# One exponential over two neighbouring PSUM banks, fewer fourth maxima and a longer lead in an attention kernel on one core

## The chip, the cores and the metric

The kernel runs on one core of a Trainium2 chip. The core has five engines that work side by side and meet at semaphores: PE (TensorE: matrix products into PSUM), DVE (VectorE), ACT (ScalarE: exponentials and other functions), POOL (GpSimd) and SP (SyncE, which issues the transfers here). PSUM has eight banks of 512 float32 columns on each of 128 partitions. The metric is the device time of one execution in microseconds (us), the median of several runs.

## The reference

Two transformer layers over 4096 rows of 256 features, 16 heads of 16. Layer 0: a block-sparse attention (each block of 128 queries sees its own 128 keys and every eighth key of the whole sequence) and a product quantised to 8 bits. Layer 1: two full causal attentions, one with rotary positions, one with normalised queries and keys, and a mixture of four experts behind the second. What bears on the change is the softmax of the causal attentions:

```python
scores = jnp.einsum('bhqd,bhkd->bhqk', Q, K) / math.sqrt(Dh)
scores = jnp.where(causal, scores, jnp.finfo(scores.dtype).min)
attn = jax.nn.softmax(scores, axis=-1)
y = jnp.einsum('bhqk,bhkd->bhqd', attn, V)
```

## The kernel before

**Units and tiles.** The 4096 queries are cut into 8 chunks of 512 (`ch`), the 16 heads into 4 groups of 4 (`g`). There are three attentions (`a`: 0 is layer 0's sparse one, 1 and 2 are layer 1's). A *unit* is one (a, g, ch). For a = 1 and 2 it runs over the keys in *tiles* of 128, 4 (ch + 1) of them; for a = 0 it has 5 tiles (four of strided keys, one of local keys).

**Scores.** In a tile the scores of the four heads stand as keys x queries, 128 x 512, each in a PSUM bank `st`. The four are made in two groups, p = 0 and p = 1, of two heads each (j = 0 and 1). Head j uses rows 64 j to 64 j + 63 of the PE array, so that the two run side by side. The softmax's row maximum is subtracted in the product itself: the first tile of a unit adds rows with the negated maxima (`pick`, `rows`), and for a = 1 and 2 the later tiles add the product with the *difference* of the keys to those before (`ke` from `e_d`). So the scores of a tile are made on top of those of the tile before, in the same bank. Each of the four banks is held for the whole unit, and a tile's product into it must await the exponential that reads the tile before. ACT makes the exponentials into SBUF tiles `pt`, 12 buffers, one instruction for each head (line 1300 in `exponentials`, 1278). `values` (1352) multiplies a tile's four `pt` with V into `po`, with 32 columns of the array for each head; in the order of the program it stands after both score groups of the next tile.

**Maxima.** The row maxima come from a second, transposed product, queries x keys, into banks `pm`, which DVE reduces to `mx`: one 128 x 512 reduction for each (query block, head, key chunk). They are made ahead, for later units, by the class `Maxima` (1098): within a score group up to two are put beside the scores, one in each half of the array (`exponentials` calls `pick` and `begin`; `emit`, 1040, takes from the two halves in turn, own scores first in the upper and last in the lower half). What isn't ready when a unit starts is made by `complete` (1232). In the stretches of the experts (`between`) `after` (1221) puts in maxima by fours.

**Who may go when.** The program's order on each engine is written out by a planner. `Clock` follows PE, DVE and ACT with prices for each operation; `pick` (1158) takes a maximum if its bank will be free, by this clock, no later than a `slack` after it could begin. `patience` (1204) gives the slack: 0.7 us if more than 2.9 maxima for each tile are still to be done in the next units, else 0.1. `LEAD` (1102) bounds how many units ahead of the one started maxima may belong to. The work of preparing and of the experts is a list with keys that say beside which tile it stands.

**PSUM.** Three rings: `max` with 3 banks, `bank` with 4, `acc` with 1 (`po`). Scores stand in `bank`; maxima beside scores in `max`; products of the preparation in `bank` unless a unit holds it, then in `max`; the experts' in `max` and the maxima beside them in `bank`. `reserve` (119) drains what is open in a ring before it hands out banks. The lines of nearly all instructions in the profile are L87, the helper that keeps the order, so groups are known by their tiles.

Of the kernel before, what the change touches and what calls it, by code (L numbers as in the profile page):

```python
# [101 lines left out]
class Schedule:  # L102
# [4 lines left out]

    RINGS = {"max": 3, "bank": 4}  # L110

    def __init__(self):
        self.items, self.n = [], 0
        self.opened = {ring: [] for ring in self.RINGS}
        self.held = 0
        self.after = None
        self.dense = False

    def reserve(self, ring, banks):
        held = self.held if ring == "bank" else 0  # L120
        while len(self.opened[ring]) + held + banks > self.RINGS[ring]:
            self.opened[ring].pop(0)[1]()

    def hold(self, banks):
        self.held += banks
# [15 lines left out]
    def run(self):  # L141
        opened = self.opened
        while self.items or any(opened.values()):
            due, ring0 = min(((min(due for due, _ in o), r) for r, o in opened.items() if o), default=(None, None))
            if not self.items or (due is not None and due <= self.items[0][0]):
                opened[ring0].pop(0)[1]()
                continue
            _, _, (ring, banks, fn, drain) = heapq.heappop(self.items)
            if ring is not None:
                ring = self.free_ring(ring)  # L150
                self.reserve(ring, banks)
            fn()
            if drain is not None:
                opened[ring].append(drain)
            self.after()


# [1 line left out]
def tile_two_layers(ctx: ExitStack, tc, d, out):  # L159
# [24 lines left out]

    sched = Schedule()

    def bank_tile(name, ring=None):
        ring = ring or sched.free_ring()
        return ps[ring].tile([P, CW], F32, tag=ring, name=name)

    def load(name, shape, dtype=F32, pool=const, src=None, eng=None):
# [23 lines left out]


    with ExitStack() as at:
        psum(at, 0, max=3, bank=4, acc=1)
        c1 = at.enter_context(tc.tile_pool(name="c1", bufs=1))
        work = at.enter_context(tc.tile_pool(name="work", bufs=1))  # L220
        clock = Clock()
# [372 lines left out]
        def prepare1(ch):  # L594
# [81 lines left out]
            for what, n, wcol, dst in (("k", 3, 1, k_d[2]), ("q", 4, 0, q_d[2])):  # L676
                z = {}
                name = what + "2"

                def mm2(tp, z=z, name=name, n=n):  # L680
                    z[tp] = bank_tile(f"p{name}{tp}{nm}").rearrange("p (t n) -> p t n", t=2)
                    for j in range(2):
                        t = 2 * tp + j
                        for c in range(2):
                            pe.matmul(
                                z[tp][:, j, :], s["ht"][:, c, t * P : (t + 1) * P],
                                w[n][:, c, :], start=(c == 0), stop=(c == 1),
                            )

                def sq2(tp, z=z, name=name):  # L690
                    if tp == 0:
                        z["raw"] = work.tile([P, TPC, E], F32, tag="xt" if name == "k2" else "cs", name=f"raw_{name}{nm}")
                        z["ss"] = small.tile([P, TPC * H], F32, tag="ss2", name=f"ss2_{name}{nm}")
                        z["rs"] = small.tile([P, TPC * H], F32, tag="rs2", name=f"rs2_{name}{nm}")
                    act.copy(z["raw"][:, 2 * tp : 2 * tp + 2], z[tp])
                    sq = work.tile([P, 2 * E], F32, tag="r1", name=f"sq2_{name}{tp}{nm}", bufs=2)
                    act.square(sq, z[tp].rearrange("p t n -> p (t n)"))
                    ss = z["ss"][:, 2 * H * tp : 2 * H * (tp + 1)]
                    dve.tensor_reduce(ss, sq.rearrange("p (h d) -> p h d", d=D), AX.X, ALU.add)

                def norms2(z=z, name=name):


                    x, y = z["ss"], z["rs"]
                    e = small.tile([P, TPC], F32, tag="ne2", name=f"ne2_{name}{nm}")
                    dve.tensor_scalar(e, s["ms"], RMS_EPS, None, ALU.mult)
                    t = small.tile([P, TPC * H], F32, tag="nt2", name=f"nt2_{name}{nm}")
                    xv = x.rearrange("p (t h) -> p t h", h=H)
                    over = e.unsqueeze(2).to_broadcast([P, TPC, H])
                    dve.scalar_tensor_tensor(xv, xv, 1.0 / D, over, ALU.mult, ALU.add)  # L710
                    dve.tensor_scalar(y.bitcast(I32), x.bitcast(I32), 1, None, ALU.logical_shift_right)
                    dve.tensor_scalar(y.bitcast(I32), y.bitcast(I32), -1, 0x5F3759DF, ALU.mult, ALU.add)
                    for _ in range(3):
                        dve.tensor_tensor(t, x, y, ALU.mult)
                        dve.scalar_tensor_tensor(t, t, -0.5, y, ALU.mult, ALU.mult)
                        dve.scalar_tensor_tensor(y, t, 1.5, y, ALU.add, ALU.mult)

                def mul2(z=z):
                    v = z["raw"].rearrange("p t (h d) -> p (t h) d", d=D)
                    dve.tensor_tensor(v, v, z["rs"].unsqueeze(2).to_broadcast([P, TPC * H, D]), ALU.mult)  # L720

                def ev2(half, pt, z=z, wcol=wcol, name=name):
                    z[half, 0] = work.tile([P, CW], F32, tag="r0", name=f"n_{name}{half}{nm}", bufs=2)
                    act.activation(z[half, 0], pt, AF.Copy, scale=qkw[:, wcol : wcol + 1])

                def st2(half, z=z, dst=dst, what=what, name=name):
                    split_stored(z[half, 0], dst, half, ch * CW, what, f"{name}{half}{nm}")

                products = [
                    (lambda tp=tp, f=mm2: f(tp), "bank", lambda tp=tp, f=sq2: f(tp)) for tp in range(2)  # L730
                ]
                turns, stores = [], []
                turn(turns, lambda z=z: z["raw"], ev2, f"pt{name}{nm}")
                for half in range(2):
                    act_piece(stores, lambda half=half, f=st2: f(half))
                    if what == "k":
                        act_piece(
                            stores, lambda half=half, z=z: steps_stored(z[half, 0], 2, ch, half, f"2{half}{nm}")
                        )
                rest.append((products, norms2, mul2, turns, stores))  # L740
# [65 lines left out]
        def experts(ch):  # L806
# [97 lines left out]

            def activated(to, func):
                def drain(f, p):
                    t = work.tile([P, CW], F32, tag="pt", name=f"h_{nm}{to}{f}", bufs=12)
                    act.activation(t, p, func)
                    s[to, f] = t

                return drain

# [185 lines left out]
        class Maxima:  # L1098


            HEADS = (1, 0, 3, 2)
            LEAD = 5

            def __init__(self):
                self.units, self.at, self.k_at, self.started = [], 0, 0, 0
# [98 lines left out]
            def patience(self, u, kt):  # L1204
# [2 lines left out]
                todo = sum(len(v["todo"]) for v in self.units[self.at : u["no"] + 1])  # L1207
                for v in self.units[u["no"] + 1 : u["no"] + 4]:
                    todo += len(v["todo"])
                    if todo > 2.9 * max(tiles, 1):  # L1210
                        return 0.7
                    tiles += (TPC * v["keys"] if v["a"] else TPC + 1) + v["spare"]
                return 0.1
# [32 lines left out]

        def neg(u):

            u["neg"] = small.tile([P, TPC * HPG], F32, tag="nm", name="nm_" + u["nm"], bufs=7)
            dve.tensor_reduce(  # L1250
                u["neg"], u["mx"][:, :, :, 0 : u["keys"]].rearrange("p t h c -> p (t h) c"), AX.X, ALU.max, negate=True
            )
# [25 lines left out]
        def exponentials(u, kt, p, lo, make, key):  # L1278
# [2 lines left out]
            if picked:  # L1281
                sched.reserve("max", len(picked))
            side, ends = stream.begin(picked, "max")
            if not u["a"]:
                sched.reserve("bank", 2)
                st = [bank_tile(f"st_{u['nm']}_{kt}_{2 * p + j}", "bank") for j in range(2)]
            elif kt == 0:
                sched.reserve("bank", 2)
                sched.hold(2)
                st = u["st", p] = [bank_tile(f"st_{u['nm']}_{2 * p + j}", "bank") for j in range(2)]  # L1290
            else:
                st = u["st", p]
            if u["a"] and kt == TPC * (u["ch"] + 1) - 1:
                sched.hold(-2)
            clock.pe = max(clock.pe, bank_ends[p])
            own = [make(st[j], j, half_rows(j)) for j in range(2)]
            emit(own[0] + side[0], side[1] + own[1])
            for j in range(2):
                pt = work.tile([P, CW], F32, tag="pt", name=f"pt_{u['nm']}_{kt}_{2 * p + j}", bufs=12)
                act.activation(pt[:, lo:], st[j][:, lo:], AF.Exp)  # L1300
                u[kt, 2 * p + j] = pt
                clock.act = max(clock.act, clock.pe + 0.2) + 0.05 + 0.43 * (CW - lo) / CW
                if j == 0:
                    bank_ends[p] = clock.act
            stream.finish(ends)

        def causal_exp(u, kt, p, key):
# [478 lines left out]
```

## Time and profile before

| | |
|---|---|
| median of 3 runs | 4914.74 us (4911.92 to 4918.79) |
| profiled execution, its own time | 4919.01 us |
| its span | 4917.2 us |
| mean granted clock of PE | 0.966 |
| PE busy | 4615.4 us |
| DVE busy | 3692.0 us |
| ACT busy | 3095.2 us, of it exponentials of scores 2581.0 in 5248 |
| PE's idle time before maxima (`pm_a`) | 135.4 us, 103.5 of it ended by DVE |
| PE's idle time before scores (`st_a`) | 31.3 us, 20.2 of it ended by ACT |

Busy time is the union of an engine's instructions; those of PE overlap each other, and the ends that the profile gives them are modelled, so a busy PE may still be waiting for part of that time. Idle time is put down to the instruction that ended it. `pt_a<-st_a` are the exponentials, `st_a<-qe_a,ke_a` the scores, `pm_a<-km_a,qm_a` the products for the maxima, `mx_a<-pm_a` their reductions, `po_a<-pt_a,v` the value products. A value product shows as two instructions for each head, eight for each tile.

### The profile page before, as it was taken

How to read it: one execution, taken by the hardware profiler on the slowest of the kernel's cores; microseconds unless marked ns; L12 is line 12 of the kernel's file. 1: busy time of each engine (PE TensorE's matmuls, PEld its weight loads, DVE VectorE, ACT ScalarE, POOL GpSimd, SP SyncE). 2: the span in 40 equal slices, each digit the busy share in tenths (PEclk: the TensorE clock that was granted, in tenths of full speed). 3: DMA queues.
4: the chain of work that ended last, by engine and by line, in shares of the span. 5: the costliest groups of instructions: out<-in, count | busy, mean ns of one | idle time of the engine just before them, and what ended most of it. 6: DMA issues, size and time to landing. Idle time of an engine off the chain costs nothing.

```text
span 4917.2 us, 83614 instructions
## 1 busy us (share of the span) xinstructions
PE 4615.4 (94%) x30176; PEld 2291.5 (47%) x30176; DVE 3692.0 (75%) x8399; ACT 3095.2 (63%) x6234; POOL 970.2 (20%) x1637
## 2 busy tenths in 40 slices
PE   6988899999999999999999999999999989999999
PEld 3544454554454445444454444444444434444435
DVE  4776687687767887888888887788887888887811
ACT  2555463477267734788358885488684678585782
POOL 2444413222222132111321103101002100000000
PEclk8988899999999999999999999999999999999999
DMA  6757656554655465444654444544344434333422
GB/s 207 233 198 271 211 188 219 192 183 167 202 176 175 163 209 176 163 160 145 216 185 150 166 145 167 183 141 159 125 148 165 170 127 148 124 131 107 132 87 77
DMA packets 532470, 822.85 MB, mean 167 GB/s; under 512 B 87380, under 2 KB 196436, under 8 KB 532056
## 3 DMA queue, kind: packets, MB, share of 16 engines
q1 hardware_dynamic: 529456, 816.12, 49.6%
q8 instruction: 239, 3.92, 0.3%
q10 hardware_dynamic: 2600, 1.39, 0.1%
q14 instruction: 175, 1.43, 0.1%
HBM read 636.45 MB, written 180.91 MB: 166 GB/s over the span
## 4 chain that ended last, share of the span: by engine, by line
PE 74%; DVE 11%; issue 6%; POOL 4%; DMA 3%; ACT 1%; SPq 0%; ACTq 0%; POOLq 0%; DVEq 0%
PE po_a L87 22%; PE st_a L87 20%; PE pm_a L87 14%; DVE mx_a L87 5%; DVE pm_a L87 3%; PE pe_m L87 2%; PE pp L87 2%; PE pq L87 2%; PE pk L87 2%; PE pv L87 1%; POOL x L87 1%; PE ph_m6l L87 1%; PE ph_m3l L87 1%; PE ph_m2l L87 1%; PE ph_m7l L87 1%
## 5 line engine op out<-in xcount | busy, mean ns | idle before, releaser
L87 ACT ACTIVATE pt_a<-st_a 128x512 f32<-128x512 f32 (+3 forms) x5248 | 2581.0, 572 | 667.0 <-PE st_a L87 423.0
L87 DVE TENSOR_REDUCE mx_a<-pm_a 128x1 f32<-128x512 f32 (+1 forms) x3712 | 2331.7, 684 | 498.5 <-PE pm_a L87 333.4
L87 PE MATMUL pm_a<-km_a,qm_a 64*128 64x512 f32 (+3 forms) x5632 | 1835.7, 432 | 135.4 <-DVE mx_a L87 103.5
L87 PE MATMUL st_a<-qe_a,ke_a 64*128 64x512 f32 (+3 forms) x5632 | 1607.6, 405 | 31.3 <-ACT pt_a L87 20.2
L87 PEld LDWEIGHTS st_a<-qe_a,ke_a 64*128 64x128 f32 x5632 | 865.2, 188 | 1072.4 <-ACT pt_a L87 963.5
L87 PE MATMUL po_a<-pt_a,v 128*32 128x512 f32 (+3 forms) x11264 | 1334.6, 552 | 0.0
L87 PEld LDWEIGHTS pm_a<-km_a,qm_a 64*128 64x128 f32 x5632 | 857.9, 189 | 528.6 <-DVE mx_a L87 370.2
L87 DVE CUSTOM_DVE_ANT_0 pm_a<-pm_a,never_sb 128x512 f32<-128x512 f32 (+3 forms) x1024 | 478.1, 518 | 231.5 <-PE pm_a L87 167.2
L87 POOL CAST rows<-tu_a 8x128 fp32r<-8x128 f32 x768 | 224.2, 292 | 1400.4 <-PE st_a L87 1023.8
L87 DVE CUSTOM_DVE_ANT_0 pm_a<-pm_a,hidden_sb 128x512 f32<-128x512 f32 x512 | 339.4, 719 | 95.4 <-PE pm_a L87 76.3
L87 PEld LDWEIGHTS po_a<-pt_a,v 128*32 128x32 f32 x11264 | 228.7, 108 | 365.5 <-issue 331.9
L87 PE MATMUL st_a<-rows,pick_r 64*128 64x512 f32 x896 | 320.5, 426 | 7.4 <-POOL rows L87 7.3
L87 POOL TENSOR_TENSOR om_a<-od_a,rd_a 128x256 f32<-128x256 f32 x96 | 60.7, 632 | 886.7 <-DVE rd_a L87 779.1
L87 PE MATMUL st_a<-mcol_sb,identb_sb 64*128 64x128 bf16 (+1 forms) x2048 | 234.9, 211 | 0.0
L87 DVE DVE_READ_ACCUMULATOR2_ANT mx_a<- 128x1 f32 x1536 | 218.3, 142 | 0.0
L87 PEld LDWEIGHTS st_a<-rows,pick_r 64*128 64x128 f32 x896 | 164.1, 193 | 18.2 <-POOL rows L87 9.0
L87 DVE STREAM_TRANSPOSE od_a<-oc_a 128x256 f32<-128x256 f32 x192 | 83.3, 434 | 90.1 <-ACT oc_a L87 89.6
L87 DVE SCALAR_TENSOR_TENSOR acc_m<-pe_m,g_wt_m,acc_m 128x192 f32<-128x192 f32 x128 | 51.5, 412 | 108.3 <-PE pe_m L87 107.6
L87 PEld LDWEIGHTS <-identb_sb 64*128 64x128 bf16 x2048 | 109.6, 97 | 19.4 <-issue 3.2
L87 POOL CAST pad<-nm_a 128x16 fp32r<-128x16 f32 x96 | 21.1, 219 | 438.1 <-DVE nm_a L87 436.8
L87 POOL TENSOR_TENSOR xa<-xa,pa 128x512 f32<-128x512 f32 (+1 forms) x48 | 57.0, 1187 | 221.0 <-ACT pa L87 138.8
L87 ACT CAST hl_e<-step 128x512 fp32r<-128x512 f32 x32 | 19.8, 618 | 126.3 <-POOL step L87 121.4
(409 smaller groups left out, 3818.3 us busy)
## 6 DMA issues: line engine op xcount, KB each, us to landing
km_a<-k_d SPq DMA_DIRECT2D x352, 512.0 KB, 3.7
ke_a<-e_d SPq DMA_DIRECT2D x288, 512.0 KB, 5.0
k_d<-hl_k SPq DMA_DIRECT2D x100, 512.0 KB, 4.4
q_d<-hl_q SPq DMA_DIRECT2D x96, 512.0 KB, 4.7
qm_a<-q_d SPq DMA_DIRECT2D x96, 512.0 KB, 5.6
qe_a<-q_d SPq DMA_DIRECT2D x96, 512.0 KB, 5.5
v<-v_d SPq DMA_DIRECT2D x352, 136.0 KB, 5.0
ke_a<-k_d SPq DMA_DIRECT2D x64, 512.0 KB, 6.0
```

What stands on the lines that cost most here:

```text
L87: got = emit(*args, **kw)
```

## The change

- The ring `bank` becomes two tiles of two neighbouring banks each (`pair_tile`). The scores of a group's two heads stand in one pair, and one ACT instruction over [128, 2, 512] makes both exponentials, into one SBUF pair `pt` (6 buffers of two instead of 12 of one). Others take a pair's halves one after the other (`bank_tile`); a half that is left when scores take a new pair is skipped. The experts' activations write into halves of a pair, too.
- `reserve` counts tiles made instead of banks held.
- The planner's price for the exponentials of a group is 0.05 + 0.79 us for 512 columns, and both banks are free at its end; it was 0.05 + 0.43 for each, and the group's banks counted as free after the first.
- `patience` gives 0.7 us only in the first two chunks of queries, and 0.1 us in all others.
- `LEAD` is 7 instead of 5, with 9 buffers for the negated maxima instead of 7. A small scratch vector of the preparation (`nt2`) has one buffer instead of two.

```diff
-    RINGS = {"max": 3, "bank": 4}
+    RINGS = {"max": 3, "bank": 2}
...
-    def reserve(self, ring, banks):
-        held = self.held if ring == "bank" else 0
-        while len(self.opened[ring]) + held + banks > self.RINGS[ring]:
-            self.opened[ring].pop(0)[1]()
+        self.made = dict.fromkeys(self.RINGS, 0)
+        self.half = None
+
+    def reserve(self, ring, banks, whole=False):
+
+        opened, new = self.opened[ring], banks
+        if ring == "bank":
+            new = 1 if whole else (banks - (self.half is not None) + 1) // 2
+        while opened and opened[0][2] + self.RINGS[ring] < self.made[ring] + new:
+            opened.pop(0)[1]()
...
+    def pair_tile(name):
+        sched.made["bank"] += 1
+        sched.half = None
+        return ps["bank"].tile([P, 2, CW], F32, tag="bank", name=name)
+
     def bank_tile(name, ring=None):
         ring = ring or sched.free_ring()
+        if ring == "bank":
+            if sched.half is None:
+                pair = pair_tile(name)
+                sched.half = pair[:, 1]
+                return pair[:, 0]
+            bank, sched.half = sched.half, None
+            return bank
+        sched.made[ring] += 1
         return ps[ring].tile([P, CW], F32, tag=ring, name=name)
...
-                    t = small.tile([P, TPC * H], F32, tag="nt2", name=f"nt2_{name}{nm}")
+                    t = small.tile([P, TPC * H], F32, tag="nt2", name=f"nt2_{name}{nm}", bufs=1)
...
-                    t = work.tile([P, CW], F32, tag="pt", name=f"h_{nm}{to}{f}", bufs=12)
-                    act.activation(t, p, func)
-                    s[to, f] = t
+                    if f % 2 == 0:
+                        t = work.tile([P, 2, CW], F32, tag="pt", name=f"h_{nm}{to}{f}", bufs=6)
+                        s[to, f], s[to, f + 1] = t[:, 0], t[:, 1]
+                    act.activation(s[to, f], p, func)
...
-            LEAD = 5
+            LEAD = 7
...
-                    if todo > 2.9 * max(tiles, 1):
+                    if u["ch"] < 2 and todo > 2.9 * max(tiles, 1):
                         return 0.7
...
-            u["neg"] = small.tile([P, TPC * HPG], F32, tag="nm", name="nm_" + u["nm"], bufs=7)
+            u["neg"] = small.tile([P, TPC * HPG], F32, tag="nm", name="nm_" + u["nm"], bufs=9)
...
-            if not u["a"]:
-                sched.reserve("bank", 2)
-                st = [bank_tile(f"st_{u['nm']}_{kt}_{2 * p + j}", "bank") for j in range(2)]
-            elif kt == 0:
-                sched.reserve("bank", 2)
-                sched.hold(2)
-                st = u["st", p] = [bank_tile(f"st_{u['nm']}_{2 * p + j}", "bank") for j in range(2)]
-            else:
-                st = u["st", p]
+            if not u["a"] or kt == 0:
+                sched.reserve("bank", 2, True)
+                u["st", p] = pair_tile(f"st_{u['nm']}_{kt}_{p}")
+                sched.hold(2 if u["a"] else 0)
+            st = u["st", p]
...
-            own = [make(st[j], j, half_rows(j)) for j in range(2)]
+            own = [make(st[:, j], j, half_rows(j)) for j in range(2)]
             emit(own[0] + side[0], side[1] + own[1])
+            pt = work.tile([P, 2, CW], F32, tag="pt", name=f"pt_{u['nm']}_{kt}_{p}", bufs=6)
+            act.activation(pt[:, :, lo:], st[:, :, lo:], AF.Exp)
             for j in range(2):
-                pt = work.tile([P, CW], F32, tag="pt", name=f"pt_{u['nm']}_{kt}_{2 * p + j}", bufs=12)
-                act.activation(pt[:, lo:], st[j][:, lo:], AF.Exp)
-                u[kt, 2 * p + j] = pt
-                clock.act = max(clock.act, clock.pe + 0.2) + 0.05 + 0.43 * (CW - lo) / CW
-                if j == 0:
-                    bank_ends[p] = clock.act
+                u[kt, 2 * p + j] = pt[:, j]
+            bank_ends[p] = clock.act = max(clock.act, clock.pe + 0.2) + 0.05 + 0.79 * (CW - lo) / CW
             stream.finish(ends)
```

More of the change, by code (lines that the diff above doesn't have):

```diff
@@ L143, in run @@
         while self.items or any(opened.values()):
-            due, ring0 = min(((min(due for due, _ in o), r) for r, o in opened.items() if o), default=(None, None))
+            due, ring0 = min(((min(due for due, _, _ in o), r) for r, o in opened.items() if o), default=(None, None))
             if not self.items or (due is not None and due <= self.items[0][0]):
@@ L153, in run @@
             if drain is not None:
-                opened[ring].append(drain)
+                opened[ring].append((*drain, self.made[ring] - 1))
             self.after()
@@ L217, in tile_two_layers @@
     with ExitStack() as at:
-        psum(at, 0, max=3, bank=4, acc=1)
+        psum(at, 0, max=3, bank=2, acc=1)
         c1 = at.enter_context(tc.tile_pool(name="c1", bufs=1))
```

## The prediction

> **What bounds the kernel now.** I read the page's busy times first, then the groups by shape, then the timeline of single tiles, and last the order in which the instructions of both programs are built.
>
> The page's first part:
>
> ```profile
> PE 4615.4 (94%) x30176; PEld 2291.5 (47%) x30176; DVE 3692.0 (75%) x8399; ACT 3095.2 (63%) x6234; POOL 970.2 (20%) x1637
> ```
>
> PE is busy 94%, but its records overlap and include waiting, so I look at the unit of work: the *tile* of 128 keys x 512 queries x four heads. A tile is a first score group E0 (pair p=0), a second, E1 (p=1), and the value products PV of the tile before. There are 1312 of them; from one E0 to the next they add up to 4900 of the 4917 us. First a tile with four maxima, then two tiles with three (PE's timeline in two stretches; start, length, both us):
>
> ```profile
> 4000.62 0.49 PE L87 MATMUL st_a<-qe_a,ke_a 64*128 64x512 f32 x1
> 4000.63 0.72 PE L87 MATMUL pm_a<-km_a,qm_a 64*128 64x512 f32 x2
> 4000.97 0.61 PE L87 MATMUL st_a<-qe_a,ke_a 64*128 64x512 f32 x2
> 4001.20 0.39 PE L87 MATMUL pm_a<-km_a,qm_a 64*128 64x512 f32 x1
> 4002.13 0.50 PE L87 MATMUL pm_a<-km_a,qm_a 64*128 64x512 f32 x1 [0.55 <-DVE mx_a L87]
> 4002.13 0.50 PE L87 MATMUL st_a<-qe_a,ke_a 64*128 64x512 f32 x1
> 4002.56 1.06 PE L87 MATMUL po_a<-pt_a,v 128*32 128x512 f32 x8
> 4003.56 0.51 PE L87 MATMUL st_a<-qe_a,ke_a 64*128 64x512 f32 x1
> ...
> 3221.30 0.49 PE L87 MATMUL st_a<-qe_a,ke_a 64*128 64x512 f32 x1
> 3221.31 0.72 PE L87 MATMUL pm_a<-km_a,qm_a 64*128 64x512 f32 x2
> 3221.64 0.79 PE L87 MATMUL st_a<-qe_a,ke_a 64*128 64x512 f32 x3
> 3222.10 0.39 PE L87 MATMUL pm_a<-km_a,qm_a 64*128 64x512 f32 x1
> 3222.42 1.07 PE L87 MATMUL po_a<-pt_a,v 128*32 128x512 f32 x8
> 3223.41 0.50 PE L87 MATMUL st_a<-qe_a,ke_a 64*128 64x512 f32 x1
> 3223.42 0.73 PE L87 MATMUL pm_a<-km_a,qm_a 64*128 64x512 f32 x2
> 3223.76 0.62 PE L87 MATMUL st_a<-qe_a,ke_a 64*128 64x512 f32 x2
> 3224.00 0.49 PE L87 MATMUL pm_a<-km_a,qm_a 64*128 64x512 f32 x1
> 3224.34 0.39 PE L87 MATMUL st_a<-qe_a,ke_a 64*128 64x512 f32 x1
> 3224.66 1.06 PE L87 MATMUL po_a<-pt_a,v 128*32 128x512 f32 x8
> ```
>
> Above, four maxima: the fourth finds its bank taken until a reduction ends, and the fourth score matmul and PV stand behind it; the tile lasts 2.94 us. Below, three maxima: PE never pauses in the first of them (2.11 us) and loses some 0.1 us in the second (2.25; its third maximum, at 3224.00, also waits for DVE). The full tiles (512 columns, nothing else in them) of the trace, by number of maxima: none, 48, mean 2.07; three, 663, mean 2.19, median 2.12; four, 61, mean 2.87. So PE bounds the tile of three, DVE the tile of four (four reductions of 0.68). ACT is the reserve; its part of a tile, from its timeline, and then two rows of the groups by shape (busy us, mean ns):
>
> ```profile
> 4004.10 2.07 ACT L87 ACTIVATE pt_a<-st_a 128x512 f32<-128x512 f32 x4 [0.80 <-PE st_a L87]
> ```
>
> ```profile
> L87 ACT ACTIVATE pt_a<-st_a 128x512 f32<-128x512 f32 x4480 | 2334.0, 604 | 528.4 <-PE st_a L87 339.5 <-PE pm_a L87 166.8
> L87 ACT ACTIVATE pt_a<-st_a 128x128 f32<-128x128 f32 x256 | 59.2, 278 | 56.2 <-PE pm_a L87 33.0 <-PE st_a L87 21.5 <-ACT pt_a L87 0.5
> ```
>
> Four exponentials take 2.07 us end to end; a column costs (604-278)/384 = 0.85 ns, 0.435 us for 512.
>
> **The change, part by part.** The sum is made on the profiled run: 4919.0 us, span 4917.2 and 1.8 around it; the median of the runs is 4.3 us lower.
>
> *No fourth maximum (patience) and lead 7.* The built orders tell where maxima move. Full tiles with none: 48 to 29; three: 663 to 742; four: 61 to 8; six and more: 16 to 11; the number of tiles is the same, 794. At the means of before (2.07, 2.19, 2.87, 2.97 for six, 3.44 for seven, 3.72 above) the 794 cost 1791 us before and 1752 after: 39 us less. First tiles of units (with row products) go 108 to 108, four maxima 82 to 79, nine and more 8 to 5: by their means (2.82 and 4.85) 5 us less; the masked tiles +3. Together **-41 us**. The maxima don't vanish: 54 fourth ones go into 19 tiles at the end that had none, where PE had room (ACT-bound, 2.07). The lead alone has no other price: more units begun means the q and k loads on SP are issued earlier, and km_a loads ended only 18.5 us of PE's idle time. Bounds: 30 us (if a freed tile costs 2.3) to 45.
>
> *One exponential for two heads.* ACT does 2624 instead of 5248. It saves one start per pair: pitch in the run of four (2.07-0.60)/3 = 0.49, minus 0.435, = 0.055 us; 145 us of ACT's time, but ACT has 0.8 us to spare in the tile above, so none of it is on the path. What counts is when a pair's banks come free. Before: the first exponential starts 0.53 after E0 (4003.56 to 4004.10), as soon as head 0's scores are done, and each bank is free for the next tile when its own exponential ends: E1's first bank 1.58 later, 2.11 after E0. After: (1) the exponential must await head 1's scores too, which stand behind a maximum in their half of the array and end 0.73 after E0 (3221.64+0.39-3221.30). (2) In the built order 2370 of the 2624 stand behind a separate wait instruction on ACT (their own buffer's last writer is a second wait; before, 1614 of 5248). In the trace an exponential that found ACT idle starts 36 ns (median of 449) after the scores' end without it and 95 ns (median of 460) with it: start 0.83. (3) Two instructions of 1024 take 2.07-0.11 = 1.96: end 2.79. (4) PE resumes 0.05 after an exponential's end (4690.75 to 4690.81 where a tile has no maxima). So **E1's first weight load of the next tile can start 2.84 after E0, where before it could at 2.16.** It is wanted at E0 + 2.18 + 0.57 - 0.11 = 2.64 (tile of three, offset of E1, weights loaded ahead). It is late by 0.2 us, and behind it in PE's order stand the maximum, head 3's scores, PV and the next E0. The late start also costs the 0.11 of loading ahead (a score matmul that begins on its weights lasts 0.50, else 0.39). From E1's late start to the E0 after it: 0.66 to PV, 1.00 to E0, 1.66. The loop spans two tiles: 2.84+1.66 = 4.50, 2.25 a tile, against 2.11 and 2.25, mean 2.18, before. DVE's 0.1 us in every second tile is swallowed by it. Price 0.06 x 635 tiles (323 and 312 of the two orders) = 40 us. For 97 full tiles whose maxima are narrower PE is faster (medians 2.08 and 2.00), E0's scores end at 0.62, the loop is (2.72+1.64)/2 = 2.18: 0.13 x 97 = 13 us. Tiles of none: 29 x -0.04 = -1. Strided, first and masked tiles have more in E0 and E1 or shorter exponentials; their E1 comes later than the release, price 0. Together **+52 us**.
>
> Bounds: below, 0 (the release is in time) less the 1 us; above, if the pair saves nothing on ACT (2.07), loop (2.95+1.66)/2 = 2.30: 76 + 18 = 94. I take 52, made of the nearest rows.
>
> The rule that speaks against the pair is in the Trainium skill, "ScalarE: Activation LUTs", What ACT_TABLE_LOAD costs: an ACTIVATE with immediate scale takes 186 ns + 0.833 ns a column, and back-to-back ones overlap by 93. The rows give 0.85 and about 0.17 fixed. By the page a pair's two would take 1.985, the loop 2.26 and the price some 61 us (an estimate): merging buys only the overlap's remainder, and delays the first half by a whole stream.
>
> *Banks in neighbouring pairs.* A preparation's product alone uses half a pair, and the next scores skip the other half. The units of layer 0 beside which products are prepared (32 tiles) may wait for an eviction more; the next scores already waited for the last exponential there: 0 to 10 us, I take 2. In the experts' stretches maxima go by fours, two pairs, and the second issued waits as before for the second reduction; six fours begin in half a pair and then wait for one of their own, at most 1.2 each, 7 us; the same stretches lose nothing else: -2 (DVE hides some) to 7, I take 2. The experts' activations write halves of a pair, as many and as long: PE's four matmuls of 0.6 hide them; were they late, one activation of 0.6 a layer. The smaller pool for one small vector and two more of another: DVE orders them itself, 0.
>
> Sum: -41 + 52 + 4 = **+15 us**: profiled 4934, median 4930.
>
> **Rivals.**
> (a) *The wait is hidden, the kernel is faster.* If the release comes by 2.64 after E0 instead of 2.84, PE is never late, and only the tiles of four count: -41 to -30, 4874 to 4885. For it: the 0.2 us rests on the start 0.30 later and a sum of four durations; PE already loses 0.1 in every second tile. Against: 0.06 of it is a wait that the order shows in nine of ten pairs. It decides from E1's weight load waiting less than 0.05 us.
> (b) *Heavier.* A pair takes as long as two and DVE's wait adds to the loop: +94-30 = +64, 4979.
> (c) *They cancel*: price 30 to 50 in the loop, gain 41: within 10 us.
>
> A change smaller than 0.2% (10 us) cannot be told from none here.
>
> **How the numbers follow.** (a) 0.30. (c) 0.20. My forecast's upper part and (b), a net loss over 10 us, 0.50. The likeliest is 4930; its own range is 4912 to 4955. The range goes from (a), 4874 less the 4 of the sum's rest, to most of (b): 4870 to 4970. Signs: faster 0.30, same 0.19, slower 0.51.
>
> **What the changed profile would show.** Full tiles of four nearly gone, PE's idle time before pm_a down from 135 us: right on the first part. Exponentials of 128x1024 at about 1.03 us, 0.83 after E0. If I am right on the second, E1's first score matmul lasts 0.50 instead of 0.39 in most tiles of three, its weight load ended by ACT pt_a, and the median of these tiles is 2.23 to 2.27. If it stays at 2.12 to 2.18, rival (a). Wrong altogether: a stage of prep or experts that changes by over 10 us.

## The result, and the profile after

| | before | after |
|---|---|---|
| median, run side by side | 4913.51 us (4 runs) | 5046.91 us (4 runs, 5042.75 to 5055.29) |
| profiled execution / its span | 4919.0 / 4917.2 us | 5046.0 / 5044.2 us |
| PE / ACT busy | 94% / 63% | 92% / 58% |

The kernel is slower: ratio 1.0272 (95% interval 1.0254 to 1.029), +133 us where the forecast was +15 (ratio 1.003, the range 4870 to 4970 us).

The first part of the page of after, and from its groups the exponentials, the products for the maxima, the scores, and the scores' weight loads (busy us, mean ns | idle time before them and what ended most of it):

```profile
PE 4658.3 (92%) x30176; PEld 2190.4 (43%) x30176; DVE 3714.1 (74%) x8399; ACT 2925.8 (58%) x3610; POOL 968.6 (19%) x1637
...
L87 ACT ACTIVATE pt_a<-st_a 128x1024 f32<-128x1024 f32 (+3 forms) x2624 | 2408.7, 961 | 893.2 <-PE st_a L87 639.8
...
L87 PE MATMUL pm_a<-km_a,qm_a 64*128 64x512 f32 (+2 forms) x5631 | 1865.1, 435 | 184.8 <-DVE mx_a L87 151.2
L87 PE MATMUL st_a<-qe_a,ke_a 64*128 64x512 f32 (+3 forms) x5632 | 1628.9, 416 | 59.8 <-ACT pt_a L87 40.1
L87 PEld LDWEIGHTS st_a<-qe_a,ke_a 64*128 64x128 f32 x5632 | 803.3, 188 | 1262.4 <-ACT pt_a L87 1094.6
```

ACT does 172 us less for the scores (2581.0 to 2408.7) and the kernel gains nothing from it. PE's idle time before maxima went from 135.4 to 184.8 us, although the fourth maxima are nearly gone; before scores from 31.3 to 59.8. So there are two new waits, one on DVE and one on ACT. To see where they are, the trace is cut into tiles, and the times from one first score to the next are added by kind of tile. The order in which each kernel was built tells which instruction belongs to which tile, so the counts differ a little from the prediction's. (us, rounded; one profiled execution of each kernel; the third column is the kernel before with patience and lead 7 alone, the run e3_pick_lead below. The expectations below give the ten stretches as 1344 and 1428 us, by another cut.)

| kind of tile | before | patience and lead, single banks | after |
|---|---|---|---|
| full tiles (814) | 1869 | 1838 | 1883 |
| first tiles of units and first masked tiles, 512 columns (102) | 293 | 294 | 292 |
| other masked tiles (172) | 373 | 370 | 372 |
| attention 2 with other work beside (23) | 144 | 143 | 144 |
| attention 1 with other work beside (31) | 156 | 153 | 151 |
| layer 0 (a = 0), with the start ahead of it | 746 | 737 | 763 |
| the ten longest stretches of the experts, with the end | 1338 | 1339 | **1438** |
| span | 4917 | 4873 | 5044 |

The full tiles did nearly what the prediction said. The experts' stretches, which it gave 2 us, take 100 us more.

**The pair's wait in the full tile.** PE's timeline of after over two tiles of three maxima (start, length, both us):

```profile
2314.25 0.50 PE L87 MATMUL st_a<-qe_a,ke_a 64*128 64x512 f32 x1
2314.25 0.73 PE L87 MATMUL pm_a<-km_a,qm_a 64*128 64x512 f32 x2
2314.59 0.73 PE L87 MATMUL st_a<-qe_a,ke_a 64*128 64x512 f32 x3
2315.16 0.39 PE L87 MATMUL pm_a<-km_a,qm_a 64*128 64x512 f32 x1
2315.48 1.06 PE L87 MATMUL po_a<-pt_a,v 128*32 128x512 f32 x8
2316.47 0.49 PE L87 MATMUL st_a<-qe_a,ke_a 64*128 64x512 f32 x1
...
2317.20 0.46 PE L87 MATMUL pm_a<-km_a,qm_a 64*128 64x512 f32 x1
...
2318.83 0.50 PE L87 MATMUL st_a<-qe_a,ke_a 64*128 64x512 f32 x1
```

ACT's timeline and that of PE's weight loads in the same stretch:

```profile
2315.11 1.94 ACT L87 ACTIVATE pt_a<-st_a 128x1024 f32<-128x1024 f32 x2 [0.35 <-PE st_a L87]
```

```profile
2317.10 0.18 PEld L87 LDWEIGHTS st_a<-qe_a,ke_a 64*128 64x128 f32 x1 [0.33 <-ACT pt_a L87]
```

The two tiles last 2.22 and 2.36 us. The first pair of exponentials begins 0.86 after E0 (2315.11 - 2314.25) and both end at 2317.05, 2.80 after E0; E1's first weights in the next tile start 0.05 later. Here the chain of the prediction can be read link by link. In 427 of the 643 tiles with three maxima of full width E1's first score matmul now lasts about 0.50; before, in 8 of 562.

**The new wait in the experts' stretches.** PE's timeline of after there, and the reductions of the four maxima in its middle:

```profile
1924.63 1.99 PE L87 MATMUL pq<-w,ht 128*128 128x256 f32 x8
1926.55 0.73 PE L87 MATMUL pm_a<-km_a,qm_a 64*128 64x512 f32 x3
1927.84 0.49 PE L87 MATMUL pm_a<-km_a,qm_a 64*128 64x512 f32 x1 [0.56 <-DVE mx_a L87]
1928.26 3.70 PE L87 MATMUL ph_m2l<-h_m2l,w_l 128*128 128x512 f32 x8
1931.89 0.73 PE L87 MATMUL pm_a<-km_a,qm_a 64*128 64x512 f32 x3
1933.17 0.49 PE L87 MATMUL pm_a<-km_a,qm_a 64*128 64x512 f32 x1 [0.55 <-DVE mx_a L87]
```

```profile
1927.09 2.48 DVE L87 TENSOR_REDUCE mx_a<-pm_a 128x1 f32<-128x512 f32 x4 [1.15 <-PE pm_a L87]
```

Of four maxima three go, and the fourth waits: the first reduction starts at 1927.09 and takes 0.68, and at 1927.84 the fourth begins. The four occupy PE from 1926.55 to 1928.26, 1.71 us. Where they pass without a wait they take 0.66, as here in the same stretch of before (1848.31 - 1847.65):

```profile
1847.65 0.73 PE L87 MATMUL pm_a<-km_a,qm_a 64*128 64x512 f32 x4
1848.31 1.57 PE L87 MATMUL pe_m<-w_e0d,h_m2e 128*128 128x192 f32 x8
```

### The profile page after: what moved, and what is told of

Same layout as the page of the kernel before. It is cut to its first block, busy times and chain, and to the rows that moved or that the text cites. A ratio compares the mean times of both kernels' runs of the same rounds, so it can differ in the third digit from the quotient of the medians.

```text
span 5044.2 us, 81693 instructions
## 1 busy us (share of the span) xinstructions
PE 4658.3 (92%) x30176; PEld 2190.4 (43%) x30176; DVE 3714.1 (74%) x8399; ACT 2925.8 (58%) x3610; POOL 968.6 (19%) x1637
## 4 chain that ended last, share of the span: by engine, by line
PE 71%; DVE 13%; issue 7%; ACT 3%; POOL 3%; DMA 2%; SPq 0%; ACTq 0%; POOLq 0%; DVEq 0%
PE st_a L87 21%; PE po_a L87 21%; PE pm_a L87 13%; DVE mx_a L87 5%; DVE pm_a L87 3%; ACT pt_a L87 2%; PE pe_m L87 2%; PE pk L87 1%; PE pp L87 1%; PE pq L87 1%; PE pv L87 1%; PE ph_m6l L87 1%; POOL x L87 1%; PE ph_m7l L87 1%; DMA k_d<-hl_k 1%
## 5 line engine op out<-in xcount | busy, mean ns | idle before, releaser
L87 ACT ACTIVATE pt_a<-st_a 128x1024 f32<-128x1024 f32 (+3 forms) x2624 | 2408.7, 961 | 893.2 <-PE st_a L87 639.8
L87 PE MATMUL pm_a<-km_a,qm_a 64*128 64x512 f32 (+2 forms) x5631 | 1865.1, 435 | 184.8 <-DVE mx_a L87 151.2
L87 PE MATMUL st_a<-qe_a,ke_a 64*128 64x512 f32 (+3 forms) x5632 | 1628.9, 416 | 59.8 <-ACT pt_a L87 40.1
L87 PEld LDWEIGHTS st_a<-qe_a,ke_a 64*128 64x128 f32 x5632 | 803.3, 188 | 1262.4 <-ACT pt_a L87 1094.6
L87 DVE CUSTOM_DVE_ANT_0 pm_a<-pm_a,never_sb 128x512 f32<-128x512 f32 x1023 | 482.5, 514 | 251.5 <-PE pm_a L87 193.5
L87 PE MATMUL st_a<-mcol_sb,identb_sb 64*128 64x64 bf16 (+1 forms) x2048 | 227.9, 211 | 0.0
```

Source lines behind the costliest of these rows:

```text
L87: got = emit(*args, **kw)
```

## The experiments

All ratios are to the kernel before, run on the same chip beside them. Its own median was 4914 us beside after, 4917 beside e1 to e4, 4919 beside e5 to e8 and 4921 beside e9, so a difference of a few us between kernels of different sets says nothing. Times by kind of tile are those of the one profiled execution of each kernel.

### e1_aligned: fours that begin with a whole pair

A run of maxima with an odd number leaves half a pair over. The next four then stand as half of X, both of Y, half of Z; the ring has two pairs, so Z is X's own pair again, and the fourth maximum waits for the reduction of the first. In the order built for after, 87 fours of the experts' stretches touch three pairs, 180 two. Edit to after:

```diff
     def emit(self, picked, ring):
+        if ring == "bank" and len(picked) > 1:
+            sched.half = None
         sched.reserve(ring, len(picked))
```

> The changed kernel, except that maxima which go several at a time into the ring of pairs begin with a fresh pair. Theory H (half pairs): in the trace of the changed kernel a group of four maxima beside the experts that touches three pair tiles lasts 1.94 us to the next instruction, one that touches two 0.87 us, and the built order has 87 groups of the first kind. With none left the experts' stretches lose 87 x 1.07 = 93 us, so 4955 (4940 to 4970), and the ten longest stretches go from 1428 us back to 1335 to 1350. Rival P (any pair is released later, whatever its alignment): the experts' stretches stay above 1400 and the time above 5025.

Measured: 4978.89 us (4973.48 to 4983.49), ratio 1.0125 (1.0105 to 1.0144), 68 us less than after. The ten stretches fall from 1438 to 1360 us, PE's idle time before maxima from 184.8 to 131.1. The same stretch in PE's timeline:

```profile
1903.12 0.73 PE L87 MATMUL pm_a<-km_a,qm_a 64*128 64x512 f32 x4
1903.78 1.99 PE L87 MATMUL pq<-w,ht 128*128 128x256 f32 x8
1905.71 0.99 PE L87 MATMUL pm_a<-km_a,qm_a 64*128 64x512 f32 x4
1906.62 3.70 PE L87 MATMUL ph_m2l<-h_m2l,w_l 128*128 128x512 f32 x8
1910.26 0.73 PE L87 MATMUL pm_a<-km_a,qm_a 64*128 64x512 f32 x4
```

The fours go in one piece. After's trace has 49 places where three go together and the fourth alone behind DVE, its start a median of 1.28 us behind the first; this kernel has none. The theory holds: 78 us for 87 fours, 0.90 each. The trace of after agrees: in the 87 the fourth matmul starts a mean of 1.33 us behind the first, in fours of two pairs 0.46. The price expected, 1.07, was too high, so the time lies above the expected 4940 to 4970. The stretches still take 21 us more than in e3; which wait makes these was not tried.

### e2_aligned_own_first: the second head's score ahead of the maximum

The pair's exponential awaits both heads of a group (j = 0 and 1), and that of j = 1 stands behind a maximum in its half of the array. The edit puts it first there. (The expectations of e6, e7 and e8 call it head 0's score; the edits move that of j = 1.) Edit to e1_aligned:

```diff
-            emit(own[0] + side[0], side[1] + own[1])
+            emit(own[0] + side[0], own[1] + side[1])
```

> As the aligned one, and both heads' scores are issued ahead of the maxima in each half of the array. Theory L (the loop over scores, exponential and release of the pair): the second head's scores end about 0.50 us after the start of a tile instead of 0.73, the pair is released 0.23 earlier, 2.61 instead of 2.84, in time for the 2.64 at which it is wanted; the median of full tiles with three maxima goes from 2.25 to 2.12-2.18 and the time falls by 45 us (30 to 60) against the aligned kernel. Rival A (the exponential itself or its longer reading of two banks costs the time): the median stays at 2.23 to 2.26 and the time within 15 us of the aligned kernel.

Measured: 4927.42 us (4916.28 to 4935.23), ratio 1.0018 (1.0007 to 1.0029), 51 us less than e1_aligned, within the 30 to 60 expected. Tiles of three fall from a median of 2.27 to 2.126 us, all full tiles from 1884 to 1806. PE's timeline:

```profile
2772.80 0.50 PE L87 MATMUL st_a<-qe_a,ke_a 64*128 64x512 f32 x2
2773.13 0.40 PE L87 MATMUL pm_a<-km_a,qm_a 64*128 64x512 f32 x2
2773.37 0.39 PE L87 MATMUL st_a<-qe_a,ke_a 64*128 64x512 f32 x2
2773.60 0.39 PE L87 MATMUL pm_a<-km_a,qm_a 64*128 64x512 f32 x1
2773.91 1.07 PE L87 MATMUL po_a<-pt_a,v 128*32 128x512 f32 x8
2774.91 0.50 PE L87 MATMUL st_a<-qe_a,ke_a 64*128 64x512 f32 x2
```

E1's scores last 0.39 again. Their exponentials begin 0.60 after E0 (median of 643 tiles; in after 0.86) and end at 2.54; with the 0.05 until PE resumes that is 2.59, just when E1 is wanted (2.13 + 0.57 - 0.11). So the pair with its full length no longer holds PE up once it starts in time. The 78 us are more than the pair's wait: the full tiles are now 32 us below those of e3, which has no pairs, in part because the score also goes past a maximum that waits for DVE (e8 tries that alone: 15 us). First tiles got longer by 7 us and layer 0 by 2 (against e1_aligned).

### e3_pick_lead: patience and lead without pairs

Edit to the kernel before: the lines of the diff for `LEAD`, `patience`, `nm` (9 buffers) and `nt2`, and nothing else.

```diff
-            LEAD = 5
+            LEAD = 7
...
-                    if todo > 2.9 * max(tiles, 1):
+                    if u["ch"] < 2 and todo > 2.9 * max(tiles, 1):
```

> The kernel before with the new patience and the lead of seven alone: single banks, one exponential for each head. If the count of tiles is what these parts are worth (61 full tiles of four maxima become 8, 48 empty ones 29), the time falls by 41 us to 4873 (4860 to 4885). Rival: the waits only move to other tiles, and the time stays within 10 us of 4914.

Measured: 4873.94 us (4865.20 to 4875.52), ratio 0.9908 (0.9891 to 0.9924). The first part of the change is worth 43 us, and the pairs with all that hangs on them cost 173 (5046.91 - 4873.94). By the table: 99 in the experts' stretches, 45 in the full tiles, 26 in layer 0, 1 in all other kinds.

### e4_two_exponentials: the pair kept, two exponentials

Edit to after; scores stay in pairs, so the next tile still waits for both:

```diff
-            act.activation(pt[:, :, lo:], st[:, :, lo:], AF.Exp)
             for j in range(2):
+                act.activation(pt[:, j, lo:], st[:, j, lo:], AF.Exp)
                 u[kt, 2 * p + j] = pt[:, j]
```

> The changed kernel with two exponentials of 512 columns on the two halves of a pair. The waits stay those of the pair: the built order shows the first exponential waiting for both heads' scores and the scores for both exponentials. Theory L: ACT takes 2.07 us instead of 1.96 for the four, the release comes 0.11 later, the loop over two tiles is 4.61 instead of 4.50, so 0.05 x 742 tiles = 40 us more than the changed kernel: 5085 (5065 to 5105). Rival A (the wide instruction is what costs): 4990 to 5010, as the tiles go back to 2.18.

Measured: 5104.79 us (5102.24 to 5110.49), ratio 1.0382 (1.0366 to 1.0399), 58 us more than after, at the top of the expected 5065 to 5105. Tiles of three go from a median of 2.27 to 2.32, all full tiles from 1883 to 1933. Four exponentials in a row end 2.93 after E0, the two of after 2.80; E1's weights in the next tile start 0.05 after that in both (medians). ACT's timeline over two tiles:

```profile
2710.44 4.20 ACT L87 ACTIVATE pt_a<-st_a 128x512 f32<-128x512 f32 x8 [0.44 <-PE st_a L87]
```

One instruction for two heads thus does save on ACT, and with a late start the pair needs that saving: both the start and the length stand in the loop. The wide instruction itself is not what costs.

### e5_pick_only and e9_lead_only: the first part taken apart

Edits to the kernel before, e5 first, then e9:

```diff
-                    if todo > 2.9 * max(tiles, 1):
+                    if u["ch"] < 2 and todo > 2.9 * max(tiles, 1):
```

```diff
-                    t = small.tile([P, TPC * H], F32, tag="nt2", name=f"nt2_{name}{nm}")
+                    t = small.tile([P, TPC * H], F32, tag="nt2", name=f"nt2_{name}{nm}", bufs=1)
...
-            LEAD = 5
+            LEAD = 7
...
-            u["neg"] = small.tile([P, TPC * HPG], F32, tag="nm", name="nm_" + u["nm"], bufs=7)
+            u["neg"] = small.tile([P, TPC * HPG], F32, tag="nm", name="nm_" + u["nm"], bufs=9)
```

> The kernel before (single banks, one exponential for each head, lead 5) with the new patience alone. Built order of the full tiles: none 41, two maxima 7, three 720, four 8 (before: 48, 0, 663, 61; with patience and lead 29, 0, 742, 8). Theory Q (the fourth maximum is the whole gain, the lead only moves maxima): by the class means of before 36 to 40 us less, about 4877, within 5 us of the run that had lead 7 too (4874). Rival (the lead brings a share of its own): half the gain or less, 4890 to 4900. Either way no change in the experts' stretches: 1344 us within 10.

> The kernel before with lead 7 and its buffers alone (old patience). Built order of the full tiles: none 37, three 699, four 40 (before 48, 663, 61). Patience alone gave 12 us where its full tiles gave 41: the rest went into maxima that were not made when their unit began. Theory T (the two need each other: patience takes the fourth maxima out, lead 7 makes room for them in time): lead alone gives what its full tiles say at the class means of before, 15 to 20 us, 4896 to 4904 beside 4914 to 4919. Rival (the lead is the whole gain of the pair of changes, 32 us or more, by itself): 4875 to 4887.

Measured: patience alone 4906.68 us (4899.06 to 4913.29), ratio 0.9971 (0.996 to 0.9982); lead alone 4893.36 (4890.09 to 4898.39), ratio 0.9939 (0.9921 to 0.9957). Neither expectation for patience alone was right. Its full tiles fall by 32 us, but two stretches of the experts grow by 22 (51.9 to 60.3 and 82.8 to 96.7 us, with 81 and 109 maxima instead of 70 and 91): what is refused beside the scores is made there. So the stretches did not stay within 10 us either. The lead alone takes 12 us off the full tiles, 6 off the stretches and 5 off layer 0; its time lies between its two expectations. In total the gains add: 12 and 28, together 40, and 43 were measured for both. By place they don't: with both, the full tiles fall by 31 and the stretches grow by only 1. So the lead does find room for what patience refuses, as theory T said, but it is worth more by itself than T gave it. How the 40 divide is uncertain: e5 was granted a lower clock, which may be some 10 of its 4907 us (last section).

### e6_single_banks_for_others: the start

After falls behind before at its start: the value products of the third unit of layer 0's second chunk begin 21 us later. PE's timeline at the start, of before, of after and of e6, which is e2 with the preparation's products and the late maxima always in the three single banks:

```profile
37.69 3.60 PE L87 MATMUL pk<-xt,ew_first 128*128 128x512 f32 x8
...
60.78 7.92 PE L87 MATMUL pm_a<-km_a,qm_a 64*128 64x512 f32 x12 [0.42 <-DVE mx_a L87]
```

```profile
46.19 3.13 PE L87 MATMUL pv<-xt,ew_first 128*128 128x512 f32 x4 [2.65 <-ACT vst L87]
...
68.59 0.79 PE L87 MATMUL pm_a<-km_a,qm_a 64*128 64x512 f32 x2 [0.65 <-DVE mx_a L87]
70.03 0.80 PE L87 MATMUL pm_a<-km_a,qm_a 64*128 64x512 f32 x2 [0.65 <-DVE mx_a L87]
```

```profile
64.75 1.44 PE L87 MATMUL pm_a<-km_a,qm_a 64*128 64x512 f32 x2 [0.20 <-DVE mx_a L87]
66.39 1.44 PE L87 MATMUL pm_a<-km_a,qm_a 64*128 64x512 f32 x2 [0.20 <-DVE mx_a L87]
```

```diff
     def free_ring(self, ring="bank"):
-        return "max" if ring == "bank" and (self.held or self.dense) else ring
+        return "max" if ring == "bank" else ring
...
-                    ring = "max" if sched.held else "bank"
+                    ring = "max"
```

> Pairs, aligned fours and head 0's score first, as in the run at 4927; in addition the preparation's products and the maxima that a unit lacks at its start always take the three single banks, never a half of a pair. Theory S (what is left of the start's loss is that products and late maxima in halves of a pair wait for a reader of the other half): the third unit of layer 0 starts 21 us later than in the kernel before in that run; here 0 to 8 later, and the time falls by 12 to 20 us, to 4907 to 4915. Rival (the start loses because three single banks are too few beside pairs, or because of the order of the maxima): the lag stays at 15 to 25 us, time 4920 to 4930.

Measured: 4908.36 us (4891.72 to 4915.36), ratio 0.9972 (0.9961 to 0.9984), 19 less than e2. The same value products begin 8 us later than before's instead of 21. So products in halves of a pair do cost at the start. The late maxima gain nothing: two take 1.64 us in the single banks (66.39 - 64.75), 1.44 in after (70.03 - 68.59), 1.32 in before (7.92 for 12). And little of the gain lasts: layer 0 falls by 13 us and the stretches by 7, but first tiles and those with other work rise by 15, and the first unit of attention 2's second chunk, whose last value product is 37 late in e2, is still 31 late here. The profiled executions of e2 and e6, both at a clock of 0.965, differ by 3 us; of the 19 between the medians some 8 may be the clock's (means 0.9637 and 0.9662; last section).

### e7_singles_selective: the order only where it helps

Edit to e6:

```diff
-            emit(own[0] + side[0], own[1] + side[1])
+            if u["a"] and kt and not lo:
+                emit(own[0] + side[0], own[1] + side[1])
+            else:
+                emit(own[0] + side[0], side[1] + own[1])
```

> The same as the run with single banks for the others, but head 0's score stands first in its half only in the tiles of attentions 1 and 2 with all 512 columns and not the first of a unit; in layer 0, in first and in masked tiles the maximum stands first again. Theory L (head 0's score first helps only where the release of the pair ends the wait): tiles of three stay at a median of 2.12 to 2.14, four maxima in layer 0 fall from 3.37 to 3.28 and first tiles from 3.01 to 2.93, together 10 to 18 us less than the run without the selection: about 4895 if that one is at 4910. Rival: those classes are set by DVE and don't move, within 4 us of it.

Measured: 4888.27 us (4883.83 to 4894.41), ratio 0.9934 (0.9919 to 0.9949), 20 less than e6. Layer 0 falls by 11 us, first tiles by 5 and tiles with other work by 7; tiles of three stay at a median of 2.127. The expectation holds. The kernel with pairs now beats the one before, but with the help of patience and lead, 43 us: it still stands 14 us behind e3, which has those and no pairs.

### e8_pick_lead_own_first: the same order without pairs

Edit to e3, single banks and two exponentials:

```diff
-            emit(own[0] + side[0], side[1] + own[1])
+            if u["a"] and kt and not lo:
+                emit(own[0] + side[0], own[1] + side[1])
+            else:
+                emit(own[0] + side[0], side[1] + own[1])
```

> The kernel before with patience and lead 7 (single banks, two exponentials, 4874) and head 0's score first in the same full tiles only. Theory D (in the tile of three the second of two tiles loses 0.1 us because its third maximum waits for DVE and head 0's score stands behind it): the score goes past the wait, tiles of three fall from a mean of 2.198 to 2.13 to 2.15, 742 of them, 30 to 45 us less, 4830 to 4845. Rival (value products or the maximum itself carry the wait on, only its place changes): mean 2.19 to 2.20, 4870 to 4878.

Measured: 4872.09 us (4867.97 to 4875.05), ratio 0.9898 (0.9881 to 0.9914), no different from e3. Tiles of three fall from a mean of 2.214 to 2.194, 15 us, less than expected and more than the rival said; first and masked tiles take as much back (9 and 7). The total is the rival's. The score does pass the waiting maximum, but little of the 0.1 us is gained by it. e3 and e8 are the fastest kernels here.

## Why the prediction was wrong

*Patience and lead, -41:* right in sum, -43 by e3, but in part by luck. The kinds of tiles that it counted (full, first, masked) gave 33 of the 44 us between the profiled executions; layer 0 gave 8 and attention 1 with other work 3, and it had put these at nothing. The statement that the lead has no other price missed that the lead alone gains 28 us, about half of it outside the full tiles, and that patience alone loses elsewhere much of what its full tiles gain.

*One exponential for two heads, +52:* right in its mechanism and nearly in size. After minus e3 in the full tiles is +45. The links measured: exponential of 128x1024 1024 ns (1.03 foretold), its start 0.86 after E0 (0.83), its pair's end 2.80 (2.79), loop over two tiles 2.20 + 2.32 = 4.52 by the medians of the two orders of a tile (4.50), median of the tiles of three 2.27 (2.23 to 2.27). (By its own numbers the loss is 2.25 - 2.18 = 0.07 a tile and 44 us, where it wrote 0.06 and 40.) e4 lengthens the pair's exponentials by 0.13 us and pays 50 us in the full tiles; e2 lets them start 0.26 earlier and gets 78 out of them, the pair's 45 and, by e8, some 15 of the rest from the same order without any pair. Rival (a), the wait is hidden, falls with it, and so does (b), by which the tiles alone would have lost 64 us. For these two terms (c) was right: 45 against 44, they cancel.

*The rule of the Trainium skill* ("ScalarE: Activation LUTs", What ACT_TABLE_LOAD costs): the prediction's estimate from it was a loop of 2.26 a tile. The measured loop is 2.26; the prediction's own rows gave 2.25, too near to tell the two apart. By the page's formula a 1024-column exponential takes 1039 ns; the groups by shape of after agree within 2%:

```profile
L87 ACT ACTIVATE pt_a<-st_a 128x1024 f32<-128x1024 f32 x2240 | 2194.9, 1024 | 733.3 <-PE st_a L87 569.1 <-PE pm_a L87 155.5 <-ACT pt_a L87 0.2
```

*Banks in neighbouring pairs, +4:* this is the step that failed. The sentence "six fours begin in half a pair and then wait for one of their own, at most 1.2 each, 7 us" had the mechanism and nearly the price, but a wrong count: 87 fours, not six, at 0.9 us, 78 of the 100 us there (e1). What it missed is that an odd run leaves half a pair for *all* fours after it, until another odd run takes that half or the next scores take a whole pair and skip it. The order built for after has eight odd runs in these stretches, and after each every four is split to the end of its stretch: in the trace they stand in whole rows, from 1898 to 2002 us one behind the other. This is also why PE's idle time before maxima rose to 184.8 us where the prediction had it fall below 135; without the split fours it is 131.1 (e1). And the preparation, "0 to 10 us, I take 2", cost some 20 at the start and 26 in layer 0: products took halves of a pair. e6 takes 13 of 21 us away there. That each product waits for the reader of the other half was read from the order, not tried by itself.

So the sum was -41 + 52 + 4 where it should have been, by the same terms, -44 + 45 + 99, 26 for layer 0 and 1 in the remaining kinds: +127, and the profiled executions differ by 127. The first two terms alone would have made it a draw. Which way the kernel went was thus decided by the term with the least work in it. The sentence "wrong altogether: a stage of prep or experts that changes by over 10 us" named the place, but no rival had been worked out for it.

What stays open: e7 stands 17 us of profiled time behind e8, by kinds of tiles 12 in the experts' stretches, 8 in layer 0, 9 in tiles with other work and 2 in first and masked tiles, with 14 gained in the full tiles. Which wait of the pair makes these was not tried.

## What to carry to other kernels

Putting two banks into one tile makes one release of two: every user of such a pair waits for the slower reader, the users that only borrow it included. Count such waits over the whole built order; a left-over half is a state that goes on, so an odd run spoils all that follow until the half is taken or skipped, and the count is not the number of odd runs. If one instruction is to serve two producers, put both producers ahead of everything else in the queue: that order took 51 us off here (e2 against e1). Even so, no kernel with pairs here reached e3 and e8, which have none.

## What was unexpected of the hardware

- One kernel's executions differ in time with the clock that PE was granted: over 36 executions of the kernel before, 0.964 (mean span 4929 us) to 0.971 (4901), by a straight line through all about 3 us for each 0.001. e5 had a mean of 0.9636 beside 0.967 of before, which by that slope is 10 of its 4907 us; e2 had 0.9637 and e6 0.9662, e3 and e9 0.968. Why kernels differ in it, and whether the change itself does it, the runs don't show.
- An exponential over two neighbouring banks costs 1024 ns; two of 512 columns cost 604 ns each but start 0.48 to 0.51 us apart (two in 1.08 to 1.09, eight in 4.20, in e4). In a row of four against two the saving is 0.13 us a tile of ACT's time (e4 against after); of the 61 us between these two profiled executions 50 stand in the full tiles, where ACT's end releases PE.
